# The beginning of a gated block: the last mixing step set ahead of the first gates, MLP pieces beside the four gates, statistics behind them

## The chip, the cores and the metric

The kernel runs on one core of one Trainium2 chip. The metric is the device time of one execution in microseconds. A core has five engines that run side by side, each with its own queue of instructions in a fixed order: TensorE (PE, matrix products into PSUM), VectorE (DVE), ScalarE (ACT, activation functions), GpSimd (POOL, which cannot read PSUM) and SyncE (SP, here the queue of the DMA transfers). An instruction starts when those before it on its engine have started and what it waits for is done.

## What is computed

Two parts follow each other, each added to its input (residual):

```python
x = x + attn_stack(layernorm(x))        # 6 layers, x is (8, 512, 128) float32
x = x + gated_block(layernorm(x))

# one layer of the stack, h of one batch is (512, 128), 16 heads of 8
q, k = h @ wq.T + bq, h @ wk.T + bk
w_avg = softmax(q_head @ k_head.T / sqrt(8)).mean(over heads)
sa = softmax(w_avg + exp(-|i - j| / 16)) @ h
h1 = ln(h + sa, ln1); h2 = ln(h1, ln2)
h = ln(h2 + relu(h2 @ w1.T + b1) @ w2.T + b2, ln3)

# the gated block, hidden width 512
g = silu((v @ w1.T) * s1) * ((v @ w2.T) * s2)      # "gates"
g = gelu((g @ h1.T) * sh1)                         # first hidden stage
g = gelu((g @ h2.T) * sh2)                         # second hidden stage
out = (g @ w3.T) * s3
```

The weights of the gated block are whole numbers -1, 0 and 1.

## The kernel before

**Units and steps.** A unit is one layer of one batch: 6 x 8 = 48 units, `U` of them, worked off one after the other. Each has 32 steps (`PAIRS`), and a step holds two score products of a head group, their peaks on DVE and their exponentials on ScalarE. All other work is hung beside these steps: `at(step, place, fn)` puts a piece into a table `later`, and `pending(step, place)` runs what stands there. A place is a spot among the instructions of a step (`P0` to `P2` beside PE's, `D0` to `D2` beside DVE's, `A0` to `A2` beside ScalarE's). So the order on each engine is written out by hand. The pieces of a unit reach far beyond it: its first two layer norms (`norm_a`, `norm_b`) run in the unit behind it, its MLP (`hidden`: four products `pf`; `mlp_out`: two halves `py`) and its last norm (`norm_c`) one unit further. When the last unit's steps are over, pieces of the last three units are therefore still in the table: the last mixing step of the last unit (`weights`, `gather` into `acc`, `mix_exp` to `w`, `mix_turn` to `pt_w`, `mix_decay` to `wT`, `mix_values` to `po`, `mix_end` to `z`), the MLP of the last unit but one, the norms and the MLP of the last. They are worked off beside the gated block.

**The gated block.** It has two arms, chosen by one value that is loaded on every engine (L1018, L1025): `gated_split` if the block's weights are exact in 12 bits, as here, and `gated` otherwise. In `gated_split` the operand of every product is cut into a high and a low part, so that two fast passes do for an exact one: `Gate.split` (L624) lets DVE cut off the low bits (L630, `cut`), POOL copy the cut part (L631, a CAST) and DVE subtract it (L632). The cut goes into one of two buffers in turn. A batch goes through four stages: stage 0, four gates (`gate_stage`: products `q1` and `q2`, Silu on ScalarE, `gt` on DVE, split into `fgs`); stage 1 and 2, the hidden stages (`hidden_stage`: eight matmuls `qh` a quarter, Gelu, and in stage 1 the split into `h1s`); stage 3, the output (`end`: `fo`, `y`). A product over the four quarters needs all four of their splits.

**The order in it.** `gated_split` loops over b: stage 0 of batch b, stage 2 of batch b - 1, the turn and the split of the next input, stage 1 of batch b with the norm of batch b + 2 beside it, stage 3 of batch b - 1. After every quarter `run_stage` calls `next_step`, which runs all pieces of the earliest step that is left in the table. `finish(upto)` runs all that are due up to a step; `norm_beside` calls it with `done(b)`, the step by which the output of batch b must be ready.

**Buffers.** All products but `acc` share a ring of 7 PSUM buffers (`ring`); a new one waits until the one 7 places earlier has been read. `gt`, `ht` and `wT` share a tag, `sil` and `w` another.

Of the kernel before, what the change touches and what calls it, by code (L numbers as in the profile page):

```python
# [17 lines left out]
P = 128  # L18
# [11 lines left out]
def attn_stack_then_ffn(ctx: ExitStack, tc: tile.TileContext, a: dict, out: bass.AP):  # L30
# [3 lines left out]
    B, L, E = x.shape  # L34
# [61 lines left out]
    def load_x(b, n):  # L96
        t = state.tile([P, LC, E], F32, tag="x", name=f"x_{n}", bufs=3)
        nc.sync.dma_start(t, x[b].rearrange("(c p) e -> p c e", p=P))
        return t
# [3 lines left out]
    def load_qk(d):  # L103
        lay_qk[d] = wts.tile([P, 2, E], F32, tag="wqk", name=f"wqk_{d}", bufs=2)
        nc.sync.dma_start(lay_qk[d], a["wqk"][d].rearrange("t e o -> e t o"))
# [29 lines left out]
    fw1 = wts.tile([P, HID], F32, name="fw1")  # L135
    fw2 = wts.tile([P, HID], F32, name="fw2")
# [5 lines left out]
    def load_ffn():  # L142
        nc.sync.dma_start(fw3, a["f_w3t"].rearrange("(c p) o -> p c o", p=P))
        nc.sync.dma_start(fw3s, a["f_w3s"].partition_broadcast(P))
# [54 lines left out]
    def ring(shape, n):  # L199
        return ps_big.tile(shape, F32, tag="big", name=n)  # L200
# [5 lines left out]
    class Norm:  # L206
        def __init__(self, src, dst, n, twice=None):


            self.src, self.dst, self.twice = src, dst, twice  # L210
            self.n = n
            self.st = small.tile([P, LC, 6], F32, tag="st", name=f"st_{n}")
# [49 lines left out]
    U = len(units)  # L262
    PAIRS = LC * STRIPS * 2
# [332 lines left out]
    class Gate:  # L596
# [2 lines left out]


        def __init__(self, b):
            self.b = b

        def add(self):
            b = self.b
# [32 lines left out]
        def products(self, ps, w, parts):  # L638

            n = len(w)  # L640
            for c in range(n):
                for k in range(2):
# [2 lines left out]
                        start=(c == 0 and k == 0), stop=(c == n - 1 and k == 1),  # L645
                    )

        def gate_stage(self):
            b = self.b
            self.parts = proj.tile([P, HC, 2, L], F32, tag="qs", name=f"fgs_{b}")  # L650
            for o in range(HC):
                sl = slice(o * P, (o + 1) * P)
                p1, p2 = ring([P, L], f"q1_{b}_{o}"), ring([P, L], f"q2_{b}_{o}")
                self.products(p1, [fw1[:, sl]], [self.vs])
                self.products(p2, [fw2[:, sl]], [self.vs])
                sil = work.tile([P, L], F32, tag="w", name=f"sils_{b}_{o}")
                nc.scalar.activation(sil, p1, AF.Silu, scale=cols["f_w1s_col"][:, o : o + 1])
                t = work.tile([P, L], F32, tag="wT", name=f"gt_{b}_{o}")
                nc.vector.scalar_tensor_tensor(
                    t, p2, cols["f_w2s_col"][:, o : o + 1], sil, ALU.mult, ALU.mult  # L660
                )
                self.split(self.parts[:, o], t, f"g{b}_{o}")
                yield
# [55 lines left out]
    gates = [Gate(b) for b in range(B)]  # L719
# [4 lines left out]
    P0, P1, P2, D0, D1, D2, A0, A1, A2, RING_ = range(10)  # L724
    later = {}

    def at(step, place, fn):
        later.setdefault((step, place), []).append(fn)
# [4 lines left out]
    def pending(step, place):  # L733
        for fn in later.pop((step, place), ()):
            fn()
# [3 lines left out]
    def matmuls(base, where, fn):  # L739

        step, place, copied, there = where
        at(base + step, place, lambda: at(base + copied, there, fn()))

    def norm_steps(base, un, make, s0, s1, s2, s3, s4):

        at(base + s0, D2, lambda: (make(), un.ln.stats(0, 2)))
        at(base + s1, D2, lambda: un.ln.stats(2, LC))
        at(base + s2, D2, lambda: un.ln.aggregate())
        if base < 0:
            at(base + s3, D2, lambda: un.ln.centre_and_scale())  # L750
            return
        at(base + s3, D2, lambda: un.ln.centre())
        at(base + s4, D2, lambda: un.ln.scale())
# [16 lines left out]
    def plan_before(un):  # L770
# [31 lines left out]
        for k in range(2):  # L802
            for lc in range(2):
                at(s + 18 + 2 * k + lc, D2, lambda k=k, lc=lc: un.mask_q(0, k, lc))
            at(s + 19 + 2 * k, D2, lambda k=k: un.stack_q(0, k))

    def plan_after(un):

        s = (un.u + 1) * PAIRS
        norm_steps(s, un, un.norm_a, 12, 12, 12, 14, 14)  # L810
        at(s + 16, D2, lambda: un.affine_a(0))
        at(s + 17, D2, lambda: un.affine_a(1))
        norm_steps(s, un, un.norm_b, 19, 19, 23, 24, 25)
        at(s + 25, D2, lambda: un.affine_b(0))
        at(s + 26, D2, lambda: un.affine_b(1))
        s += PAIRS
        places = ((11, P1, 12, A1), (13, P2, 14, D1), (18, P2, 19, A1), (14, P2, 14, A1))
        for f, where in enumerate(places):
            matmuls(s, where, lambda f=f: un.hidden(f))
        for half, (st, p, sd, q) in enumerate(((22, P2, 23, D0), (30, P1, 30, D1))):  # L820
            at(s + st, p, lambda half=half: un.mlp_out(half))
            at(s + sd, q, lambda half=half: un.mlp_add(half))
        norm_steps(s, un, un.norm_c, 28, 31, 31, 39, 41)
        at(s + 43, D2, lambda: un.affine_c(0))
        at(s + 44, D2, lambda: un.affine_c(1))
# [14 lines left out]
    def step_rest(s):  # L840
        for k in range(9):
            pending(s, k)

    def step_ring(s):
        for fn in later.pop((s, RING_), ()):
            fn()()
# [17 lines left out]
    def load_out(b):  # L864
        if b < 2:
            xs[b] = load_x(b, f"out{b}")
        elif b < B:
            tag = ("hik", "lok", "hiq", "z1")[b % 4]
            bufs = None if tag == "z1" else 1
            shape = [P, LC, EW] if tag == "z1" else [P, LC, E]  # L870
            xs[b] = work.tile(shape, F32, tag=tag, name=f"x_out{b}", bufs=bufs)[:, :, 0:E]
            nc.sync.dma_start(xs[b], x[b].rearrange("(c p) e -> p c e", p=P))
# [3 lines left out]
    for b in range(2):  # L876
        gate, t = gates[b], (U - 2 + b) * PAIRS
        at(t - 4, D2, lambda b=b: load_out(b))
        at(t + 9, D2, gate.add)
        at(t + 14, D2, lambda gate=gate: gate.ln.stats(0, 2))  # L880
        at(t + 15, D2, lambda gate=gate: gate.ln.stats(2, LC))
        at(t + 26, D2, lambda gate=gate: gate.ln.aggregate())
        at(t + 28, D2, lambda gate=gate: gate.ln.centre())
        at(t + 29, D2, lambda gate=gate: gate.ln.scale())
    for u, un in enumerate(obj):
        un.z1 = work.tile([P, LC, EW], F32, tag="z1", name=f"z1_{un.n}")
        if u + 2 < B:
            x_in[u + 2] = load_x(u + 2, f"in{u + 2}")
        if un.b == 4 and un.d + 1 < D:
            load_qk(un.d + 1)  # L890
            load_layer(un.d + 1)
        if u == 0:
            load_layer(0)
        if u == U - B:
            load_ffn()
        if u + 2 < U:
            plan_before(obj[u + 2])
        plan_turns(u)
        plan_after(un)
        for pr in range(PAIRS):  # L900
            s = u * PAIRS + pr
            lc, turn, half = pr // 8, (pr // 2) % STRIPS, pr % 2
            if half == 0:
                gr = Group(un, lc, turn, gr)
                recent = [*recent[-3:], gr]
            pend = lambda k: pending(s, k)
            if half == 1:
                plan_group(gr, s)
            pend(P0)
            peak, exps = gr.scores(half, pend)  # L910
            pend(P2)
            pend(D0)
            peak()
            pend(D2)
            pend(A0)
            exps(pend)
            pend(A1)
            pend(A2)
            step_ring(s)
# [3 lines left out]
    def finish(upto):  # L923

        for s in sorted({s for s, _ in later}):
            if s <= upto:
                step_rest(s)
                step_ring(s)
# [6 lines left out]

    def done(b):

        return (U - B + b + 4) * PAIRS + 12

    def gated(b):  # L940

# [35 lines left out]
    def run_stage(b, k, beside=()):  # L977

        beside = iter(beside)
        if 0 <= b < B:  # L980
            for _ in gates[b].stage(k):
                next(beside, lambda: None)()
                next_step()
        for fn in beside:
            fn()

    def norm_beside(b):
# [9 lines left out]
            lambda: gate.ln.scale(),  # L997
        )

    def gated_split():  # L1000

        load_out(2)
        load_out(3)
        gates[0].split_input()
        for b in range(B + 1):
            run_stage(b, 0)
            run_stage(b - 1, 2)
            if b + 1 < B:
                if b + 1 > 1:
                    gates[b + 1].turn(ring([P, L], f"pt_w{b + 1}"))()  # L1010
                gates[b + 1].split_input()
            run_stage(b, 1, norm_beside(b + 2))
            run_stage(b - 1, 3)
            if b > 0:
                load_out(b + 3)
# [9 lines left out]
    with tc.If(wide < 1) as narrow:  # L1025
        gated_split()
# [65 lines left out]
```

## Time and profile before

| | us |
|---|---|
| median of 3 runs (lowest, highest) | 2605.64 (2603.69, 2607.17) |
| the profiled execution, device time | 2605.65 |
| its span, first to last instruction | 2603.9 |

| engine | busy us | share of the span |
|---|---|---|
| PE | 2523.6 | 97% |
| DVE | 2490.0 | 96% |
| ScalarE | 2449.8 | 94% |
| POOL | 1829.5 | 70% |

The steps of the 48 units end near 2385 us of the span; the gated block takes the rest, some 219 us. A page of a profile gives the busy time of each engine in 40 equal slices, a chain of waits and groups of instructions. Other views give, for a stretch that one asks for, the busy time of each engine in windows (the columns are: window, its length, busy time with the number of instructions for PE, PE's weight loads, DVE, ScalarE and POOL, the granted clock of PE, the DMA share and GB/s), what an engine waited for (total, times, longest), and the instructions in order of time (start, duration, engine, line, operation, out<-in, and in brackets the idle time ahead with what ended it).

### The profile page before, as it was taken

The numbers are of one execution on the slowest core, as the hardware profiler recorded it, in microseconds if no ns is written. First come the engines' busy times: TensorE is split into PE (matmuls) and PEld (weight loads), VectorE is DVE, ScalarE is ACT, GpSimd is POOL, SyncE is SP. The second block draws the span as 40 slices with busy tenths as digits, with TensorE's granted clock in tenths as the row PEclk, the third lists the DMA queues.
The fourth block names the chain that finished last, engine by engine and source line by source line (L and its number), as shares of the span: only waits on it lengthen the run. The fifth ranks groups of instructions, "written<-read, shape, count | busy, mean of one in ns | idle before, by whom it ended". The sixth has DMA issues, their size and how long they took to land.

```text
span 2603.9 us, 51821 instructions
## 1 busy us (share of the span) xinstructions
PE 2523.6 (97%) x14944; PEld 1436.8 (55%) x14944; DVE 2490.0 (96%) x5582; ACT 2449.8 (94%) x6798; POOL 1829.5 (70%) x1984
## 2 busy tenths in 40 slices
PE   5899999999999999999999999999999999998998
PEld 2455555555555555555555555555555555555787
DVE  7999999999999999999999999999999999998874
ACT  5999999999999999999999999999999999998443
POOL 3667777767767767767777777777777777775974
PEclk7999999999999999999999999999999999999999
DMA  6554544545444545544445445445445545541000
GB/s 167 122 119 119 118 102 110 114 103 126 114 101 111 114 99 130 114 99 113 114 97 132 114 94 117 112 98 133 113 96 122 129 117 136 133 104 36 9 25 18
DMA packets 137299, 276.38 MB, mean 106 GB/s; under 512 B 39857, under 2 KB 57393, under 8 KB 137009
## 3 DMA queue, kind: packets, MB, share of 16 engines
q1 hardware_dynamic: 136432, 272.23, 44.8%
q8 instruction: 121, 1.98, 0.3%
q14 instruction: 170, 1.38, 0.2%
q10 hardware_dynamic: 576, 0.79, 0.1%
HBM read 16.48 MB, written 2.10 MB: 7 GB/s over the span
## 4 chain that ended last, share of the span: by engine, by line
PE 52%; ACT 31%; DVE 9%; issue 3%; POOL 3%; SPq 1%; DMA 1%; DVEq 0%; POOLq 0%; ACTq 0%
ACT e L535 26%; PE ps L515 16%; PE acc L557 15%; DVE top L526 6%; PE py L472 5%; PE po L583 4%; PE qh L643 4%; PE pt_w L252 2%; ACT w L565 2%; PE pf L452 1%; PE pk L295 1%; PE fo L689 1%; ACT qT L305 1%; ACT kT L296 1%; ACT g L460 1%
## 5 line engine op out<-in xcount | busy, mean ns | idle before, releaser
L535 ACT ACTIVATE e<-ps,top 128x512 f32<-128x512 f32 x3072 | 2141.3, 821 | 24.7 <-DMA ks_first<-lok 11.5
L526 DVE TENSOR_REDUCE top<-ps 128x1 f32<-128x512 f32 x3072 | 1924.4, 678 | 25.3 <-PE ps L515 20.7
L515 PE MATMUL ps<-ks,qs 128*128 128x512 f32 x3008 | 1140.6, 469 | 12.9 <-ACT e L535 10.8
L535 ACT ACTIVATION_READ_ACCUMULATOR e<-ps,top 128x1 f32 x3072 | 1043.2, 340 | 0.0
L515 PEld LDWEIGHTS ps<-ks,qs 128*128 128x128 f32 x3008 | 518.7, 189 | 611.2 <-ACT e L535 308.3
L557 PE MATMUL acc<-e,rp 128*32 128x512 f32 x6144 | 741.4, 600 | 0.0
L557 PEld LDWEIGHTS acc<-e,rp 128*32 128x32 f32 x6144 | 160.5, 109 | 331.0 <-issue 330.5
L546 POOL TENSOR_TENSOR rp<-pick,r 128x256 f32<-128x256 f32 x384 | 237.4, 618 | 127.5 <-DVE r L544 89.2
L356 POOL TENSOR_TENSOR m<-hiq,mask 128x512 f32<-128x512 f32 x190 | 241.6, 1283 | 3.3 <-DMA qs_first<-m_first 3.3
L356 POOL TENSOR_TENSOR m<-loq,mask 128x512 f32<-128x512 f32 x190 | 241.6, 1284 | 2.4 <-DMA qs_first<-m_first 2.4
L583 PEld LDWEIGHTS po<-h,wT 128*128 128x128 f32 x1536 | 200.7, 191 | 18.0 <-issue 0.6
L583 PE MATMUL po<-h,wT 128*128 128x129 f32 x1536 | 202.4, 275 | 0.0
L452 PE MATMUL pf<-uT,w 128*128 128x512 f32 x384 | 195.9, 591 | 0.9 <-ACT ht L679 0.9
L314 POOL TENSOR_TENSOR loq<-qT,hiq 128x512 f32<-128x512 f32 x47 | 60.3, 1283 | 187.2 <-DVE hiq L313 176.5
L472 PEld LDWEIGHTS py<-w,g 128*128 128x128 f32 x1536 | 186.2, 192 | 8.4
L472 PE MATMUL py<-w,g 128*128 128x128 f32 x1536 | 186.9, 275 | 0.0
L252 PE MATMUL pt_w<-ident,w 128*128 128x128 f32 x768 | 120.7, 280 | 22.0 <-ACT e L535 13.7
L565 ACT ACTIVATE w<-acc 128x512 f32<-128x512 f32 x192 | 136.9, 713 | 0.3 <-PE acc L557 0.3
L575 DVE TENSOR_TENSOR wT<-pt_w,decay 128x512 f32<-128x512 f32 x192 | 130.3, 679 | 0.0
L252 PEld LDWEIGHTS pt_w<-ident,w 128*128 128x128 f32 x768 | 87.9, 140 | 75.1 <-ACT e L535 55.3
L460 ACT ACTIVATE g<-pf,b_col 128x512 f32<-128x512 f32 x144 | 127.9, 888 | 0.2 <-PE pf L452 0.2
L228 POOL TENSOR_TENSOR rs_c<-mv_c,eps 128x4 f32<-128x4 f32 x48 | 9.7, 203 | 166.1 <-DVE mv_c L222 166.1
(125 smaller groups left out, 2651.7 us busy)
## 6 DMA issues: line engine op xcount, KB each, us to landing
qs<-m SPq DMA_DIRECT2D x1520, 128.0 KB, 2.4
ks<-hik SPq DMA_DIRECT2D x376, 64.0 KB, 2.0
ks<-lok SPq DMA_DIRECT2D x376, 64.0 KB, 2.0
rows<-in_rows SPq DMA_DIRECT2D x6, 448.0 KB, 4.8
x_in<-in_x SPq DMA_DIRECT2D x8, 256.0 KB, 2.9
fh<-square SPq DMA_DIRECT2D x8, 256.0 KB, 2.3
x_out<-in_x SPq DMA_DIRECT2D x8, 256.0 KB, 2.9
out<-y SPq DMA_DIRECT2D x7, 256.0 KB, 2.4
```

What stands on the lines that cost most here:

```text
L252: nc.tensor.transpose(pt[:, c * P : (c + 1) * P], src[:, c, :], ident)
L356: nc.gpsimd.tensor_tensor(m[:, lc - 2 * two], part.unsqueeze(2).to_broadcast([P, NB, PER_STRIP, QB]), mask.unsqueeze(1).to_broadcast([P, N ...
L452: nc.tensor.matmul(pf, w1[:, f * P : (f + 1) * P], self.uT, start=True, stop=True)
L460: nc.scalar.activation(self.g[:, f, :], pf, AF.Relu, bias=cols["b1_col"][:, k : k + 1])
L472: nc.tensor.matmul(self.py[:, k, :], self.g[:, f, c * P : (c + 1) * P], w2[:, f, :], start=(f == 0), stop=(f == FC - 1),)
L515: nc.tensor.matmul(ps[s], qs[:, nb * P : (nb + 1) * P].bitcast(F32R), un.ks[:, i, :].bitcast(F32R), start=True, stop=True,)
L526: nc.vector.tensor_reduce(top[s], ps[s], AX.X, ALU.max, negate=True)
L535: nc.scalar.activation(self.e[:, nb, :], ps[s], AF.Exp, bias=top[s], accum_out=self.zs[:, i % 2, nb : nb + 1],)
L546: nc.gpsimd.tensor_tensor(self.rp.rearrange("p t n l -> p (t n) l"), pick.unsqueeze(1).to_broadcast([P, 2 * NB, QB]), r.rearrange("p t n - ...
L557: nc.tensor.matmul(acc[nb * QB : (nb + 1) * QB, :], self.rp[:, gr.turn % 2, nb, :], gr.e[:, nb, :], start=(gr.turn == 0), stop=(gr.turn == ...
L565: nc.scalar.activation(self.w.rearrange("p c l -> p (c l)"), acc, AF.Exp, scale=1.0 / H)
L583: nc.tensor.matmul(self.po, self.wT[:, c, :], self.unit.h[:, c, 0 : E + 1], start=(c == 0), stop=(c == LC - 1),)
```

## The change

Five places of the gated block's beginning are changed.

- `split_input` of batch 0 is put into the table at the last step of the last unit, place `D2`, so it stands ahead of the branch; before it stood behind it.
- The products of a gate become a method of their own, `gate_products`, which keeps them in a list `ahead`; `gate_stage` takes them from there if there are any.
- `gated_split` begins with the products of gate 0, then all pieces up to 6 steps behind the last unit (`weights`, `gather`, `mix_exp`), the products of gate 1, and all pieces up to 9 steps (`mix_turn`, `mix_decay`). Behind gate 0 the pieces up to 10 steps follow (`mix_values`, `mix_end`). Before, one step was taken after each gate.
- After each of the four gates of batch 0 `mlp_ahead` runs one `hidden` product `pf` of the last unit but one, with its relu, ahead of its turn. The places of the four are named `HIDDEN`.
- `done(b)` is one unit (32 steps) less, so `norm_beside` no longer empties the table one unit beyond what the batch needs.

From there on `next_step` takes one step after each quarter as before, from a table in which other steps are left; the norms of the last unit and the second half of its MLP so come beside other stages than before.

```diff
         def __init__(self, b):
-            self.b = b
+            self.b, self.ahead = b, []
...
+        def gate_products(self, o):
+            b, sl = self.b, slice(o * P, (o + 1) * P)
+            p1, p2 = ring([P, L], f"q1_{b}_{o}"), ring([P, L], f"q2_{b}_{o}")
+            self.products(p1, [fw1[:, sl]], [self.vs])
+            self.products(p2, [fw2[:, sl]], [self.vs])
+            self.ahead.append((p1, p2))
+
         def gate_stage(self):
...
             for o in range(HC):
-                sl = slice(o * P, (o + 1) * P)
-                p1, p2 = ring([P, L], f"q1_{b}_{o}"), ring([P, L], f"q2_{b}_{o}")
-                self.products(p1, [fw1[:, sl]], [self.vs])
-                self.products(p2, [fw2[:, sl]], [self.vs])
+                if not self.ahead:
+                    self.gate_products(o)
+                p1, p2 = self.ahead.pop(0)
...
+    HIDDEN = ((11, P1, 12, A1), (13, P2, 14, D1), (18, P2, 19, A1), (14, P2, 14, A1))
...
+    at(U * PAIRS - 1, D2, gates[0].split_input)
...
     def done(b):
 
-        return (U - B + b + 4) * PAIRS + 12
+        return (U - B + b + 3) * PAIRS + 12
...
+    def mlp_ahead(f):
+
+        step, place, copied, there = HIDDEN[f]
+        pending(U * PAIRS + step, place)
+        pending(U * PAIRS + copied, there)
+
     def gated_split():
 
         load_out(2)
         load_out(3)
-        gates[0].split_input()
+
+        gates[0].gate_products(0)
+        finish(U * PAIRS + 6)
+        gates[0].gate_products(1)
+        finish(U * PAIRS + 9)
         for b in range(B + 1):
-            run_stage(b, 0)
+            if b == 0:
+                for f, _ in enumerate(gates[0].stage(0)):
+                    finish(U * PAIRS + 10)
+                    mlp_ahead(f)
+            else:
+                run_stage(b, 0)
             run_stage(b - 1, 2)
```

More of the change, by code (lines that the diff above doesn't have):

```diff
@@ L816, in plan_after @@
         s += PAIRS
-        places = ((11, P1, 12, A1), (13, P2, 14, D1), (18, P2, 19, A1), (14, P2, 14, A1))
-        for f, where in enumerate(places):
+        for f, where in enumerate(HIDDEN):
             matmuls(s, where, lambda f=f: un.hidden(f))
```

## The prediction

> **What bounds the kernel now.** I read the page's slices first, then what TensorE (PE) waits for in the stretch that the diff touches, then the stretch in windows, then the clock, then GpSimd's (POOL) rows.
>
> ```profile
> PE   5899999999999999999999999999999999998998
> DVE  7999999999999999999999999999999999998874
> POOL 3667777767767767767777777777777777775974
> ```
>
> All engines are full through attention; only the last four slices, some 220 us, differ. There ScalarE and VectorE (DVE) loosen and POOL rises to 9: this is the gated block with the last MLPs beside it.
>
> ```profile
> PE qh L643 <- POOL fgs L631: 3.5, 2, 1.8
> PE q L643 <- POOL vs L631: 2.4, 1, 2.4
> PE q L643 <- ACT sils L657: 1.0, 1, 1.0
> PE pf L452 <- ACT ht L679: 0.9, 1, 0.9
> PE q L643 <- DVE y L696: 0.2, 1, 0.2
> ```
>
> This is all that PE waits for from 2384 to 2450: 8.0 us, of which 5.9 is for POOL's casts (its part of each hi/lo split).
>
> ```profile
> 2380.00:2400.00 20.00, 14.67 (x96) 9.18 (x94) 14.79 (x32) 13.50 (x26) 11.03 (x13) 1.00 0.00 0
> 2400.00:2425.00 25.00, 22.48 (x85) 16.04 (x86) 17.23 (x39) 12.22 (x17) 18.38 (x21) 0.93 0.00 1
> 2425.00:2450.00 25.00, 24.78 (x141) 20.61 (x141) 20.87 (x47) 9.14 (x13) 23.09 (x23) 1.00 0.01 1
> 2475.00:2500.00 25.00, 25.00 (x127) 20.84 (x126) 20.15 (x39) 11.89 (x16) 22.02 (x22) 1.00 0.04 12
> ```
>
> The second column is PE's busy time, the fifth POOL's, the sixth the clock. From 2444 PE is busy without a break until 2593. So PE's idle time ahead of 2444 is all that can be won, and POOL, at 23.1 of 25 us, is nearly full just there.
>
> ```profile
> 2401.00:2402.00 1.00, 1.00 (x3) 0.73 (x3) 0.87 (x2) 1.00 (x1) 0.69 (x1) 0.50 0.06 16
> 2402.00:2403.00 1.00, 1.00 (x4) 0.79 (x3) 0.00 (x0) 0.20 (x1) 0.38 (x1) 0.50 0.00 0
> 2403.00:2404.00 1.00, 1.00 (x4) 0.81 (x3) 0.00 (x0) 0.00 (x0) 0.00 (x0) 0.50 0.00 0
> ```
>
> PE's clock is halved from about 2400.75 to 2404.2, 3.4 us, which costs 1.7. In the 3.4 us ahead of it PE had worked 0.85.
>
> **The ledger.** The change adds no matmul, so the time moves by what PE loses. Before it loses 2.42 + 1.80 + 1.75 + 0.90 + 0.98 + 0.22 = 8.07 idle (the gaps of its timeline) and 1.7 by the clock: 9.8 us. Now the same for the order in which the changed program stands on each engine, each step with durations of the trace before. PE's prices, start to start: a gate's pair of products 0.94, one hidden product (8 matmuls) 1.88, one `pf` 0.86, `po` 0.81, `acc` 1.85, `py` 1.78.
>
> **1. The split of v ahead of the branch.** The last peak ends at 2384.09; cut 0.43 and POOL's cast 1.07 give the first gate its operand at 2385.65, just as `acc` ends (2385.64): the wait of 2.42 goes. The branch may hold PE 0 to 0.6 (DVE's gap there is 0.60; I take 0.1). What is pushed back is DVE's queue: 0.43 + 0.69 ahead of the statistics (0.39 + 0.29), `wT` and the reciprocal, and POOL's `rs_c` (0.25 + 1.02) and `rp` (0.62) behind them, so `rp` ends at 2387.95, where PE, through with the first pair and `po`, is ready at 2387.45. Loss 0.1 + 0.5.
>
> **2. The last mixing step ahead of the gates.** `acc` to 2389.85, `w` 0.60, transposes, `wT` 0.68 to 2392.1; PE has the second pair to fill this and is out of work at 2391.2. Loss 1.0. Won: two of ScalarE's table loads (1.28 each), since `w` now uses the table that is loaded.
>
> **3. Four gates with the MLP pieces beside them.** The first `gt` writes where `wT` stood and must wait for `po`: 2393.3. A gate costs DVE 2.14 (2395.62 to 2397.76 in the trace); `z` 0.26 and the `g` on DVE 0.66 now stand between, so the fourth `gt` starts at 2393.3 + 3 x 2.14 + 0.92 = 2400.6 and its cast ends at 2403.0. PE, from 2393.0, has four `pf` (3.44), two pairs (1.88) and six of the eight first matmuls (1.4): to 2399.7. Loss 3.3. So far 4.9 against 5.97 before.
>
> **4. The hidden stage of batch 0.** `ht` waits for the split of the one before; in the trace they lie 2.04, 3.48 and 2.09 apart. Now `st_f`, `st_a` and `mv_a` (0.78 + 0.78 + 0.29) all stand ahead of the third split, which makes the last some 3.1: from 2403.8 the fourth `ht` ends at 2413.1. `py`, which follows three gate pairs, takes its PSUM buffer; PE is there at 2411.9. Loss 1.2.
>
> **5. POOL's queue behind it.** In the trace these rows stand between the third and the fourth cast of the hidden stage:
>
> ```profile
> 2412.55 1.14 POOL L631 CAST h1s<-cut_h 128x512 fp32r<-128x512 f32 x1 [0.97 <-DVE cut_h L630]
> 2413.65 0.20 POOL L228 TENSOR_TENSOR rs_f<-mv_f,eps 128x4 f32<-128x4 f32 x1
> 2413.92 1.02 POOL L229 TENSOR_TENSOR rs_f<-rs_f,neg_half 128x4 f32<-128x4 f32 x1
> 2414.92 1.26 POOL L232 TENSOR_TENSOR v<-x_out,mv_f 128x512 f32<-128x512 f32 x1
> 2416.14 1.27 POOL L487 TENSOR_TENSOR z<-z,rows 128x512 f32<-128x512 f32 x1
> 2417.36 0.60 POOL L631 CAST h1s<-cut_h 128x512 fp32r<-128x512 f32 x1
> ```
>
> Earlier statistics put more there: `h` L489 (1.73) and the four of `least_a`/`rs_a` (2.44) ahead of the third cast, and `rs_f`, centre, centre again and scale (1.27 + 1.26 + 1.22 + 1.37) ahead of the fourth. From the second cast's end at 2409.7 (5.9 after the first `ht`, as before): third 2415.0, fourth 2420.7. PE, after `py`, a pair and six matmuls, needs it at 2417.4. Loss 3.3.
>
> **6. Gates of batch 1.** The cut buffers are two, so the second gate's cut waits for that fourth cast; DVE then stands before `st_b`, which needs `z` L424, POOL's fifth row after it (1.04 + 1.46 + 0.6 + 1.29: 2425.0). Two gates follow: last cast 2430.2. PE is ready at 2428.6. Loss 1.6.
>
> **7. `py` of the last unit** now stands two products into batch 1's second hidden stage and needs the `g` that DVE makes after its third split, whose cut waits for POOL's first cast. Ahead of that cast stand v's scale, `z` L245, `y` and L487 (1.04 + 1.48 + 1.56 + 1.29); before, only v's scale and `y` stood there. Loss 3.3. Small gaps, 0.6.
>
> The DMAs (SP's two `x_out` loads of 256 KB) keep their order and land 2.7 us after issue, against needs 20 us later: nothing.
>
> **The sum.** 0.6 + 1.0 + 3.3 + 1.2 + 3.3 + 1.6 + 3.3 + 0.6 = 14.9. Laying out the kernel before in the same way gives 9.3 idle where the trace has 8.07, so I take off 1.2. The clock: halved once in the trace, after 0.85 us of work in 3.4; the gaps of steps 3, 5 and 7 are of that kind, and it depends on where they fall in the clock's window, so none to three trips at 1.7; I take one. 14.9 - 1.2 + 1.7 - 9.8 = +5.6. The profiled execution took 2605.65 (span 2603.9 and 1.75 around it), the runs' median is 2605.64: **2611 us**.
>
> [...]
>
> Bounds: steps 5 to 7 rest on POOL's times, which in the trace go from 0.56 to 1.14 for a cast and from 1.04 to 1.5 for a centre or scale, as DVE works beside it. With the short ones all three vanish (-8.2); with the long ones they grow by some 3.
>
> **The rivals.**
> *POOL keeps up* (not slower). If casts and scales take the short times, steps 5 to 7 cost nothing and no clock trips: 14.9 - 8.2 - 1.2 - 9.8 = -4.3, 2601. For it: POOL idles 2.8 and 4.6 us at a time around 2390 and 2405, so work pulled forward has room. Against: the change fills that room only in part, and in 2425-2450 POOL is 92% busy with the long times in most rows. It decides from where the fourth cast of step 5 ends before 2417.4.
> *The clock trips at all three gaps* (slower still). 14.9 - 1.2 + 5.1 - 9.8 = +9, 2614.7. For it: each gap leaves a 3.4 us window with under 0.9 us of work at some phases. Against: the phase is chance.
> *It does not do what it says at its head*: PE cannot pass the branch before 2388 whatever lies ready. The gap stays 2.4, gates follow as laid out: +5.6 + 1.8 = 2613. Against: ScalarE passed the branch with 0.02 us between `vT` and its table load.
>
> **How the numbers follow.** This kernel's measurement tells 0.2%, 5.2 us, from no change. Steps 5 to 7 as laid out, with none to two trips (+3.9 to +7.3, 2609.5 to 2613): 0.55, of which 0.20 lies inside 5.2 us. Three trips or a closed head (over +7.3): 0.13. POOL keeps up, wholly or for the most part: 0.32, of which 0.10 is over 5.2 us faster. So faster 0.10, same 0.42, slower 0.48. The range leaves out about 0.12 below and 0.08 above: 2601 to 2615.
>
> **What would show it.** Right: `q` starts within 0.7 us of `acc`'s end; waits of PE for POOL's `h1s` casts near 3 us, absent before; `py` waiting for DVE; POOL over 90% busy from 2405. Wrong: PE gaps under 10 us in all up to the end of batch 1, or the fourth `h1s` cast done before PE asks for it; a waiting queue that I put on POOL lying on DVE or ScalarE.

## The result, and the profile after

| | before | after |
|---|---|---|
| median of 13 runs (lowest, highest), us | 2605.12 (2603.69, 2608.12) | 2615.16 (2611.69, 2617.57) |
| the profiled execution, us | 2605.65 | 2617.57 |
| its span, us | 2603.9 | 2615.8 |
| PE idle from 2384 us to the last product, us | 8.07 | 11.95 |
| PE lost by a halved clock there, us | 1.71 | 8.53 |

The kernel became slower by 10.0 us, a ratio of 1.0034 [1.0027, 1.0041]. The last two rows are the prediction's ledger read once more; the clock's loss is 1 less the granted clock, summed over windows of 1 us. Their sum went from 9.8 to 20.5, which is +10.7. So the time is where the ledger looked for it: 3.9 of it is idle time, 6.8 is clock. The profiled execution is the slowest of the 13 runs, and only its idle part repeats: a second profile of the same program (run 8 below) has +4.9 idle and +1.7 by the clock.

What PE waits for from 2384 to 2602 (total, times, longest):

```profile
PE py L472 <- DVE g L456: 4.5, 1, 4.5
PE qh L643 <- POOL fgs L631: 4.5, 5, 1.4
PE qh L643 <- POOL h1s L631: 2.2, 1, 2.2
PE po L583 <- DVE wT L575: 0.8, 1, 0.8
```

The wait for the first split (2.4, `q <- POOL vs`) is gone, and with it those for `sils`, `ht` and `y`. Three waits are new: the last mixing step's `po`, the fourth `h1s` cast, and `py` of the last unit, the longest of all.

The same stretch in windows (behind the window and its length the busy times of PE, PE's weight loads, DVE, ScalarE and POOL, then the granted clock):

```profile
2380.00:2400.00 20.00, 19.09 (x117) 12.27 (x113) 13.89 (x33) 13.59 (x30) 11.36 (x13) 1.00 0.00 1
2400.00:2425.00 25.00, 20.32 (x78) 15.19 (x77) 18.85 (x37) 10.36 (x13) 21.50 (x23) 0.86 0.00 0
2425.00:2450.00 25.00, 24.62 (x129) 19.33 (x128) 18.64 (x46) 10.48 (x15) 20.71 (x22) 1.00 0.00 1
2450.00:2475.00 25.00, 20.50 (x93) 16.98 (x92) 12.20 (x19) 7.16 (x10) 13.87 (x13) 0.86 0.08 22
2475.00:2500.00 25.00, 23.40 (x112) 18.90 (x111) 20.11 (x37) 10.52 (x14) 20.80 (x21) 0.93 0.08 22
```

The first line has what was won: PE is busy for 19.09 of 20 us, before for 14.67. A part of that is only moved, since the change's waits at the gates (1.09 + 1.41) lie behind 2400: up to the first hidden product PE idles 3.28, before 5.97. The fourth and fifth lines have what it cost. Before, PE was busy there for 25.00 of 25 at full clock; the fourth line of the kernel before is

```profile
2450.00:2475.00 25.00, 25.00 (x139) 20.61 (x138) 18.61 (x33) 11.98 (x18) 21.33 (x22) 1.00 0.11 31
```

Now PE idles 4.5 and 1.6, and the clock falls. POOL's work has moved forward: it is fuller in the second line (21.50, before 18.38), less full in the third (20.71, before 23.09) and far less in the fourth (13.87, before 21.33), where the longest wait lies. So it isn't short of time there; its rows come in another order.

What happens around the longest wait, in windows of 1 us:

```profile
2457.00:2458.00 1.00, 0.00 (x0) 0.00 (x0) 0.96 (x2) 0.00 (x0) 1.00 (x2) 1.00 0.44 132
2459.00:2460.00 1.00, 0.49 (x2) 0.49 (x3) 1.00 (x2) 0.00 (x0) 0.27 (x1) 0.50 0.00 0
2462.00:2463.00 1.00, 1.00 (x6) 1.00 (x5) 0.10 (x1) 0.00 (x0) 0.00 (x0) 0.50 0.00 0
2465.00:2466.00 1.00, 1.00 (x4) 0.77 (x4) 0.00 (x0) 0.00 (x0) 0.00 (x0) 0.66 0.00 0
```

PE stands still, then works at half clock, from about 2458.9 to 2465.7: two halved stretches of 3.4 us in a row, 3.4 lost. Three others lie behind the other gaps: 2404.2 to 2407.7 (behind 1.09 + 1.41 idle at the gates), 2421.3 to 2424.7 (behind 2.18 for the `h1s` cast) and 2496.4 to 2499.8 (behind 0.20 + 1.41 at the hidden stage of batch 3).

Why `py` waits, in VectorE's rows in order of time (start, duration, out<-in, idle time ahead with what ended it):

```profile
2453.48 0.75 DVE L665 SCALAR_TENSOR_TENSOR gt<-q,f_w2s_col,sils 128x512 f32<-128x512 f32 x1
2456.31 1.47 DVE L630 TENSOR_SCALAR cut_g<-gt 128x512 int32<-128x512 int32 x1 [2.08 <-POOL fgs L631]
2457.82 0.98 DVE L632 TENSOR_TENSOR fgs<-gt,cut_g 128x512 fp32r<-128x512 f32 x1
2458.72 0.74 DVE L456 TENSOR_SCALAR g<-pf,b_col 128x512 f32<-128x512 f32 x1
```

The third cut needs the buffer that POOL's first cast has not read, because `v`, `z`, `y` and `z` again (1.04, 1.22, 1.74, 1.26) stand ahead of that cast. DVE stands for 2.08, and the relu `g`, whose operand has long been there, is queued behind it. PE starts `py` at 2454.63 with two matmuls, then waits until 2459.51.

The wait for `h1s`, in POOL's rows ahead of it:

```profile
2413.78 1.23 POOL L229 TENSOR_TENSOR rs_a<-rs_a,neg_half 128x4 f32<-128x4 f32 x1
2414.75 0.69 POOL L631 CAST h1s<-cut_h 128x512 fp32r<-128x512 f32 x1
2415.41 0.64 POOL L228 TENSOR_TENSOR rs_f<-mv_f,eps 128x4 f32<-128x4 f32 x1
2416.13 1.01 POOL L229 TENSOR_TENSOR rs_f<-rs_f,neg_half 128x4 f32<-128x4 f32 x1
2417.10 1.05 POOL L232 TENSOR_TENSOR v<-x_out,mv_f 128x512 f32<-128x512 f32 x1
2418.11 1.23 POOL L232 TENSOR_TENSOR z<-z,mv_a 128x512 f32<-128x512 f32 x1
2419.41 1.37 POOL L245 TENSOR_TENSOR z<-z,rs_a 128x512 f32<-128x512 f32 x1
2420.73 0.61 POOL L631 CAST h1s<-cut_h 128x512 fp32r<-128x512 f32 x1
```

Before, four rows stood between the last two casts, the last of them a `z` of 1.27; now there are five, and the last two are another `z`'s centre and scale (2.60 us), since the table now holds other steps when `next_step` is called. Ahead of the third cast, too, `h` and the rows of `least_a` and `rs_a` have come in: its cut is ready at 2412.91, the cast starts at 2414.75. The fourth cast ends 2.1 us after PE asks for it.

### The profile page after: what moved, and what is told of

It reads as the page before. It is cut to its first block, busy times and chain, and to the rows that moved or that the text cites. A ratio compares the mean times of both kernels' runs of the same rounds, so it can differ in the third digit from the quotient of the medians.

```text
span 2615.8 us, 51824 instructions
## 1 busy us (share of the span) xinstructions
PE 2532.9 (97%) x14944; PEld 1443.1 (55%) x14944; DVE 2488.1 (95%) x5582; ACT 2447.8 (94%) x6796; POOL 1829.8 (70%) x1984
```

## The experiments

Theory A is the prediction's account: the new order puts POOL's and DVE's rows ahead of casts and of a relu that PE needs, and each gap can halve the clock behind it. Its rival, theory C, puts the loss on the work pulled to the four gates itself. Each expectation says what the theories give. The kernel before was run beside them: 2605.41 us with the first four, 2604.49 with the others. The ratios are taken against these.

**1. No halved clock.** 40 matmuls are added that write the bank of `acc`, which is not read any more by then: 8 ahead of the first hidden product of batch 0, 9 ahead of its second hidden stage, 18 ahead of the last unit's first `py`, 5 in batch 3.

```diff
+    def keep_busy(n, vs):
+        for _ in range(n):
+            nc.tensor.matmul(
+                acc, fw1[:, 0:P].bitcast(F32R), vs[:, 0, :].bitcast(F32R), start=True, stop=True
+            )
...
+    BUSY = {("h1", 0, 0): 8, ("h2", 0, 0): 9, ("py", 0): 18, ("h1", 3, 0): 5}
...
         def mlp_out(self, half):
             w2 = lay[self.d][1]
+            if narrow_arm and self.u == U - 1:
+                keep_busy(BUSY.get(("py", half), 0), gates[2].vs)
...
             for o in range(HC):
+                keep_busy(BUSY.get((nm, b, o), 0), self.vs)
```

> The changed kernel with 40 matmuls more on PE (about 0.23 us each, 9.4 us in all; they write the bank of acc, which nobody reads any more), set ahead of the four products at which PE stood idle: 8 ahead of the first hidden product of batch 0, 9 ahead of its second hidden stage, 18 ahead of the last unit's first py, 5 ahead of the first hidden product of batch 3. What is computed is the same. Theory A (half of the loss is the clock, which halves behind each gap: five windows of 3.4 us, 8.5 us, against one, 1.7 us, before): with PE kept busy the clock stays full and the time falls by 4 to 8 us, to 2607-2611, though PE has 9.4 us more to do. Theory B (the clock only follows, the loss is the waiting itself): nothing is won, 2615-2617, and more if the added work delays what follows.

Measured: 2609.68 us, ratio 1.0017 [1.0008, 1.0026]. The two windows in which the clock fell most:

```profile
2400.00:2425.00 25.00, 23.02 (x104) 17.72 (x103) 19.48 (x37) 10.68 (x14) 22.43 (x23) 1.00 0.00 0
2450.00:2475.00 25.00, 24.64 (x129) 20.59 (x128) 15.00 (x32) 7.85 (x11) 15.02 (x15) 1.00 0.08 22
```

The clock stays full; 40 useless matmuls make the kernel 4 to 5 us faster than the change (2609.68 against 2615.16; by the ratios, 1.0017 against 1.0034). PE's idle time falls to 5.17, and the matmuls take 40 x 0.235 = 9.4 (eight of one hidden product take 1.88). 5.17 + 9.4 - 9.8 = +4.8, where +4.4 was measured. Of the 9.4 us of added work 6.8 took the place of idle time (11.95 to 5.17), and the 8.53 that the clock lost in the first profile are gone.

**2. One relu on the other engine.** The last unit's second relu, the `g` that `py` waits for, goes to ScalarE.

```diff
-                if f == 1:
+                if f == 1 and self.u < U - 1:
                     nc.vector.tensor_scalar(
```

> The changed kernel with one edit: the relu of the last unit's second MLP piece on ScalarE and not on DVE, so that the py which PE reaches in batch 1's second hidden stage no longer needs an instruction that stands behind the third gate's split on DVE. Theory A (py waits only for that relu; its 4.5 us and the two half-clock windows behind it, 3.4 us, go): 2607-2609. Theory B (POOL is late as a whole and the wait only moves to the next product over all four splits): 2612-2615, with a PE wait for fgs casts of 3 us or more some 6 us later.

Measured: 2605.23 us, ratio 1.0000 [0.9991, 1.0009].

```profile
PE qh L643 <- POOL fgs L631: 4.2, 4, 1.4
PE qh L643 <- POOL h1s L631: 2.2, 1, 2.2
PE py L472 <- ACT ht L685: 1.0, 1, 1.0
PE po L583 <- DVE wT L575: 0.8, 1, 0.8
```

The wait of `py` for `g` is gone, the wait for `h1s` is as it was. One instruction of 0.74 us that changes its queue brings 8 to 10 us (1.0000 against the change's 1.0034 and, in run 8, 1.0031; 2605.23 against 2615.16), more than theory A gave. Against the first profile, 3.8 us less are idle (4.5 gone; 1.0 for `ht`, at the `py` of the last unit but one, has come), and the clock loses 6.8 less: the two halved stretches behind the wait are gone, and two more, at the gates and at batch 3. Nothing shows those two to be the relu's doing: they stood behind the same gaps as here (1.09 + 1.41, and 1.40), behind which the clock stayed full this time, as it did in run 8. In this profile it is halved once, behind the `h1s` gap.

**3. One step held back.** `next_step` isn't called in stage 1 of batch 0, so the pieces behind it come up to four steps later.

```diff
-                next_step()
+                if (b, k) != (0, 1):
+                    next_step()
```

> The changed kernel, but no step of the table is taken in batch 0's first hidden stage, so that the last unit's first norm and what follows come four steps later, as late as before the change. Head, mixing step and MLP pieces stay as changed. Theory A (statistics on POOL ahead of the casts make the gaps): the waits for the h1s cast (2.2 us) and for the relu of py (4.5 us) and their clock windows go, 2603-2606. Theory C (the MLP pieces beside the gates and the mixing step ahead make the loss, the statistics do nothing): 2613-2616.

Measured: 2601.14 us, ratio 0.9984 [0.9975, 0.9993].

```profile
PE qh L643 <- POOL fgs L631: 3.9, 3, 1.4
PE q L643 <- DVE y L702: 1.5, 1, 1.5
PE po L583 <- DVE wT L575: 0.8, 1, 0.8
```

The waits for `h1s` and for `g` have both gone: `z`'s centre and scale no longer stand between the last two casts (the fourth starts at 2412.40, behind `rs_f` and `v` alone), and the last unit's `py`, at 2458.48, comes 4.3 us behind the end of its relu, which now stands behind the fourth gate's subtraction (2453.40). All pieces at the gates are as in the change. So what costs is not those pieces, but where the steps after them fall: theory C falls, A holds, though the time lies 2 us below the range that A gave. The clock is halved once (1.70).

**4. The first part alone.** The kernel before, with nothing but the split of batch 0 set ahead of the branch.

```diff
+    at(U * PAIRS - 1, D2, gates[0].split_input)
...
         load_out(2)
         load_out(3)
-        gates[0].split_input()
         for b in range(B + 1):
```

> The kernel before with one part of the change: the split of batch 0's input ahead of the branch. Nothing else moves. Theory A (step 1 of the prediction: the wait of 2.42 us goes and some 0.1 to 0.6 come back): 2602.5-2604. Theory D (the branch holds PE, or the wait comes back at the first hidden product): 2605.

Measured: 2601.57 us, ratio 0.9986 [0.9977, 0.9995]. PE's gap of 2.42 is gone, the others are as before (1.93, 1.75, 0.90, 0.98, 0.22), the clock's loss is 1.71. The time is 1 us below what theory A gave. This one line is worth as much as the whole change with its steps held back (run 3): pulling the last mixing step and the MLP pieces ahead brought nothing that the measurement can tell.

**5. The casts of batch 0's hidden stage on ScalarE**, so POOL's statistics no longer stand ahead of them.

```diff
-            nc.gpsimd.tensor_copy(dst[:, 0, :].bitcast(F32R), m)
+            if n.startswith("h0_"):
+                nc.scalar.copy(dst[:, 0, :].bitcast(F32R), m)
+            else:
+                nc.gpsimd.tensor_copy(dst[:, 0, :].bitcast(F32R), m)
```

> The changed kernel with the four h1s casts of batch 0 on ScalarE and not on POOL; every statistic keeps its place on POOL. Theory A (the fourth cast is late because POOL's queue stands in front of it): PE's wait of 2.2 us for it goes, and with it a half-clock window (1.7); the wait of py, which hangs on POOL's work later on, stays over 3 us. 2610-2613. Theory E (the split itself is late, on DVE or behind its activation): the wait stays, now for ScalarE or DVE, 2614-2617.

Measured: 2612.09 us, ratio 1.0028 [1.0018, 1.0038]. The `h1s` wait of 2.2 is gone, and the 4.50 of `py` stands untouched: the two are separate causes. But nothing is won that the measurement can tell from the change (run 8: 1.0031 [1.0020, 1.0043]): a wait for `sils` of ScalarE (1.06) has come, and the one at batch 1's first hidden stage grew from 0.38 to 1.41, so PE idles 11.64 in all, in the change 11.95.

**6. No MLP pieces beside the gates.** One step of the table is taken there instead, from the second gate on.

```diff
-                    mlp_ahead(f)
+                    if f:
+                        next_step()
```

> The changed kernel without the MLP pieces beside the four gates: after the second to fourth gate one step of the table is taken, as before the change. Split, first products and mixing step stay ahead. Theory A (the loss sits in what the table brings forward for POOL, and the steps that are now taken beside the gates bring the last unit's norm forward too, while PE has less to do beside the gates): 2609-2616, with a wait at the first hidden product longer than the changed kernel's 2.5 us. Theory C (the MLP pieces on DVE and ScalarE delay the gates and so make the loss): 2601-2605.

Measured: 2607.10 us, ratio 1.0009 [1.0000, 1.0018], between what the theories gave. Without them PE idles longer at batch 0's first hidden stage (0.69 + 1.99 + 3.53 = 6.2, with them 2.5), as A said. But neither the 4.5 of the last unit's `py` nor the 2.2 of `h1s` arises; only a wait of `py` for ScalarE's `g` comes in (1.85, at 2416.18), and the 1.40 at batch 3 stays. The last unit's relu stands one gate earlier in VectorE's queue, behind the second gate's subtraction (2450.50) and ahead of the third cut, the one that waits for POOL. So the 4.5 belongs to one place: a gate earlier (here) or behind all four gates (run 3) it is gone. I had charged this kernel with it, so A's number was too high, while the pieces themselves fill 3.7 us at the gates.

**7. Run 3 with 6 of the matmuls of run 1** ahead of the first hidden product.

```diff
+    BUSY = {("h1", 0, 0): 6}
...
-                next_step()
+                if (b, k) != (0, 1):
+                    next_step()
```

> Run e3 (no step of the table in batch 0's first hidden stage) with 6 matmuls more (1.4 us) ahead of the first hidden product, where PE waited 1.09 + 1.41 us and the clock then halved. What is computed is the same. Theory A: the clock stays full, 1.7 us less, 2599-2600.5, though 1.4 us of work is added. Theory B (the clock only follows): 2601-2602.5.

Measured: 2602.18 us, ratio 0.9989 [0.9980, 0.9998]. The clock stays full at the gates, as theory A had it, but the time is not the one that A gave: 2602.18 is in theory B's range, and the interval overlaps that of run 3 for the most part. No gain is shown. 1.7 saved stands against 6 x 0.235 = 1.4 of added work, and PE's idle time falls by 0.5 only (6.24 to 5.75).

**8. The change again**, unaltered, on the chip of runs 5 to 7.

> The changed kernel once more, unaltered, to see what in its profile repeats. Theory A: the gaps of PE come back within 0.3 us each (they follow from the order), the half-clock windows need not (where a gap falls in the clock's window is chance): between two and five of them, and the runs' times spread by more than the 4 us of the kernel before, 2611-2618. Theory B: gaps and windows are the same each time.

Measured: 2612.98 us, ratio 1.0031 [1.0020, 1.0043].

```profile
2400.00:2425.00 25.00, 20.98 (x88) 16.34 (x89) 19.49 (x40) 10.03 (x13) 22.05 (x24) 0.93 0.00 0
2450.00:2475.00 25.00, 20.49 (x111) 17.69 (x110) 13.10 (x34) 6.41 (x11) 13.41 (x14) 0.93 0.08 22
2475.00:2500.00 25.00, 23.40 (x120) 19.03 (x119) 20.27 (x32) 11.23 (x16) 21.52 (x22) 1.00 0.08 22
```

The gaps are those of the first profile within 0.04 us (0.78, 1.10, 1.41, 2.18, 0.34, 4.51, 0.20, 1.40), and one of 1.01 ahead of the last but one unit's `py` comes in. The clock's loss is 3.42 instead of 8.53: two stretches, not five. The idle time belongs to the order of the program; how often the clock falls behind it changes from one execution to the next. The times spread by 4.7 us, as those of the kernel before do; theory A had expected more. Attention too ended elsewhere: `po` starts at 2390.21 here, at 2393.24 in the first profile. So spans of single profiles can't be set against each other within some 3 us, but the ledger of gaps and clock can.

What changes is where the clock falls behind these gaps, and for how long:

| profile | clock halved from | for, us | PE worked in the 3.41 us ahead |
|---|---|---|---|
| first | 2404.24 | 3.4 | 1.11 |
| first | 2421.30 | 3.4 | 1.32 |
| first | 2458.85 | 6.8 | 0.00 |
| first | 2496.39 | 3.4 | 1.81 |
| run 8 | 2419.14 | 3.4 | 1.25 |
| run 8 | 2456.69 | 3.4 | 0.68 |

Up to the end of the gates' two gaps PE worked 0.91 of 3.41 us in the first profile, and the clock fell 0.38 us later; in run 8 it worked 0.90, and the clock stayed full. `py` begins again 0.66 us after the clock has fallen in the first profile, where it stays halved for 6.8 us; in run 8 it begins 0.7 ahead of the fall, which lasts 3.4. So these gaps do not by themselves tell whether the clock falls, nor for how long; what decides it was not shown.

The ledger of all runs, in us, against the measured ratio:

| kernel | PE idle | clock | added matmuls | sum - 9.8 | ratio x 2605, less 2605 |
|---|---|---|---|---|---|
| the change, first profile | 11.95 | 8.53 | 0 | +10.7 | +8.9 |
| the change again | 12.93 | 3.42 | 0 | +6.6 | +8.1 |
| 1 no halved clock | 5.17 | 0.00 | 9.4 | +4.8 | +4.4 |
| 2 relu on ScalarE | 8.20 | 1.71 | 0 | +0.1 | 0.0 |
| 3 step held back | 6.24 | 1.70 | 0 | -1.8 | -4.2 |
| 4 split ahead alone | 5.78 | 1.71 | 0 | -2.3 | -3.6 |
| 5 casts on ScalarE | 11.64 | 5.13 | 0 | +7.0 | +7.3 |
| 6 no MLP pieces | 10.25 | 5.11 | 0 | +5.6 | +2.3 |
| 7 step held back, 6 matmuls | 5.75 | 0.00 | 1.4 | -2.6 | -2.9 |

It is off by at most 3.3 us, about what one or two halved stretches of the one profiled execution make.

The edit of `done(b)` plays no part: alone, on either kernel, it leaves the order of the instructions on every engine as it was.

## Why the prediction was right, and where not

The direction and the mechanism held: of the waits that it laid out the larger ones are there, on the engines that it named, and the clock falls behind them. The size did not hold as well. +5.6 us was forecast, +10.0 measured by the medians and +8.9 by the ratio; that is at the upper end of the range (2601 to 2615), and what lies over +7.3 had been given only 0.13. The mis-sized term is the clock, "none to three trips at 1.7; I take one": five halved stretches of 3.4 us in the first profile, two in the second, so 8.5 and 3.4 us instead of 1.7. That a trip depends on where a gap falls "in the clock's window" was my assumption; the runs show only that the clock fell behind a gap in one execution and not behind the same gap in another. Two of the five lie behind a single gap, and one behind a gap that I had not laid out. What a typical execution loses by the clock is not known from two profiles. An estimate from run 1, where the clock stays full, is 5 to 7 us: by the ratios it is 3.6 to 4.4 us faster than the change, though its idle time and added matmuls (14.6) come to 1.6 to 2.6 more than the change idles. The idle time came out a little below the forecast, in part by luck: steps 1 to 6 were priced too high, the last `py` and the small gaps, those at batch 3 among them, too low.

| step | forecast | first profile | again |
|---|---|---|---|
| 1 split ahead of the branch | 0.6 | 0 | 0 |
| 2 last mixing step | 1.0 | 0.78 | 0.78 |
| 3 four gates | 3.3 | 2.50 | 2.51 |
| 4 `py` of the last unit but one | 1.2 | 0 | 1.01 |
| 5 fourth `h1s` cast | 3.3 | 2.18 | 2.18 |
| 6 gates of batch 1 | 1.6 | 0.38 | 0.34 |
| 7 `py` of the last unit, for `g` | 3.3 | 4.50 | 4.51 |
| small gaps | 0.6 | 1.61 | 1.60 |
| sum (forecast: less 1.2) | 13.7 | 11.95 | 12.93 |
| clock | 1.7 | 8.53 | 3.42 |

- Step 1: the branch held PE for nothing that shows, and `rp` was there when PE asked for it. Run 4 gives the price: the 2.42 of the gap, and nothing taken back.
- Step 3: `gt` waits for `po` (1.31 of DVE's idle time), as laid out, and the gates follow each other at 2.12, 2.58 (with the relu `g` between) and 2.14 us: 6.84 for the three, laid out as 7.34. The clock halved there in the first profile, though not in runs 2 and 8 behind the same two gaps.
- Step 4 is missing in the first profile because the clock was halved just ahead of it: PE came later. The halved clock paid back a part of itself in that wait: in the second profile, at full clock, the wait is 1.01, in run 2 it is 1.02, and in run 5, where the clock was halved at that place, there is none.
- Step 5: attention ended 1.1 us later in this execution than in the one that the prediction laid out. Less that, the third cast ended at 2414.3 (laid out 2415.0) and the fourth at 2420.2 (2420.7), and PE came at 2418.1 (2417.4), behind a halved stretch; in run 8, without that stretch, it came at 2417.6. Both shorten the wait.
- Step 6: 0.4 instead of 1.6. Step 5's shorter wait was carried into it, and the statistics did not hold the casts of those gates for long.
- Step 7: DVE behind POOL's first cast, as laid out, but longer: 2.08 of waiting for POOL, then a cut of 1.47 and a subtraction of 0.98, where 0.43 and 0.69 are the short times. Run 2 shows the place: the same relu in ScalarE's queue has no wait.
- Two readings ahead of the steps were off, though neither enters the sum: POOL is not full through attention (its slices stand at 6 and 7 tenths), and in the lines of windows POOL is the sixth number and the clock the seventh.
- The gaps of 0.20 and 1.41 at batch 3's hidden stage were not foreseen. The 1.4 is in runs 2, 5, 6 and 8 (0.7 of it in run 1, beside added matmuls) and gone in runs 3 and 7; what is late there on POOL was not settled.

To count trips at gaps of 3.3 us and less was right for this kernel: a gap of 2.18 us with work on both sides is followed by a halved stretch in the first profile and in runs 2 and 8, and so is 1.09 + 1.41 us with 0.7 of work between in the first profile. Nor did PE stand idle for the whole 3.41 us ahead of each fall: of the 14 falls in the ten profiles, between 2384 and the last product, only one, in the 4.5 of `py`, came after 0.00 us of work; ahead of the others PE had worked 0.68 to 1.81.

Of the rivals, "POOL keeps up" did not come: `h1s` and `g` are late, and POOL's short cast of 0.61 changed nothing as the rows ahead of it stand anyway. "The clock trips at all three gaps" (2614.7) came nearest to the median, and I gave it too little, because I thought of one trip a gap at most and of each as the toss of a coin. Its condition was met in the first profile, but not in the second, where the gates' gaps tripped nothing. "It does not do what it says at its head" is refuted by run 4. The sign "POOL over 90% busy from 2405" was wrong too: it is 86% and 83% busy in the two windows from 2400, less than before in the second. The other signs came: `q` starts 0.03 us behind `acc`, `h1s` is waited for (2.2), `py` waits for DVE.

## What to carry to other kernels

Work that is pulled ahead in a hand-made order pulls everything behind it ahead as well: price the later steps by what stands in front of them in each queue, not by how busy the engine is. A short instruction behind one that waits on another engine can cost many times its own length (here 4.5 us of idle time for 0.74, and the clock behind it), and moving it to another queue, or holding the table back by a step, is the cheap repair. Where a profile shows the clock halved behind idle stretches, take its loss as an amount with a spread, not as a single number (here 8.53 and 3.42 us in two profiles of one program).

## What the runs showed of the hardware

- In the ten profiles PE's clock fell to half 14 times between 2384 us and the last product, 11 times for 3.4 us and three times for 6.8. In the 3.41 us ahead of a fall PE had worked 0.00 to 1.81 us; in run 8 it had worked 0.90 up to 2400.84, and the clock stayed full.
- The same program lost 8.53 and 3.42 us by the clock with gaps that agree within 0.04 us, apart from the one of step 4, and a gap of 4.5 us was followed by 6.8 us of halved clock in the first profile and by 3.4 in run 8.
- Matmuls of no use put in front of the waits (run 1) went with a full clock in the whole block: 0.00 us lost in the one profile of it, in the change 8.53 and 3.42.
- VectorE's cut took 0.43 us with POOL idle (at 2400.04) and 1.47 beside POOL's two-operand `h` and the `fgs` cast (2456.31 in the rows above). Its subtraction took 0.69 beside a cast of POOL (at 2400.50) and 1.41 beside `z` and `y` there (at 2451.94).
